# 98 of 8832 row tiles of a recommender kernel fetched row by row from ScalarE's queue

## The chip, the core and the metric

The kernel runs on one core of a Trainium2 chip. A core has five engines with instruction streams of their own: TensorE (PE), VectorE (DVE), ScalarE (ACT), GpSimd (POOL) and SyncE (SP). TensorE multiplies matrices and writes into PSUM. VectorE and ScalarE do elementwise work. DMAs between HBM and the on-chip memory are issued by GpSimd, SyncE or ScalarE and are carried by the core's 16 DMA engines. Engines wait for each other through semaphores. The metric is the time of one execution on the device in microseconds; lower is better.

## The reference

16384 samples have 69 item numbers each, and one label. Each item number picks a row of 96 float32 from a table of 100001 rows. Each row is weighted by a small network that looks at the row, the label's row and their difference and product; the weighted rows are summed in ten groups of fields (20, 20, 10, 10, 2, 2, 2, 1, 1, 1), and a network of three layers turns the sums into one number for each sample.

```python
u = emb[batch_user]
ql = emb[batch_label[:, 0]]
q = jnp.broadcast_to(ql[:, None, :], u.shape)
z = jnp.concatenate([q, u, q - u, q * u], axis=-1)
h = _dice(z @ W1 + b1, a1, EPS_DICE)
h = h @ W2 + b2
att = h @ W3 + b3
eff = (batch_user < ITEM_NUM)[..., None]
pre = jnp.where(eff, u * att, 0.0)
pooled = jnp.einsum('gf,bfe->bge', window, pre).reshape(u.shape[0], G * E)
x = jnp.concatenate([pooled, ql], axis=-1)
h = _dice(_bn_eval(x @ Wf1 + bf1, EPS_BN), af1, EPS_DICE)
h = _dice(_bn_eval(h @ Wf2 + bf2, EPS_BN), af2, EPS_DICE)
return h @ Wf3 + bf3
```

`_dice(x, a)` is (a (1 - p) + p) x with p the sigmoid of x. The 16384 x 69 = 1130496 picked rows are fetched as 8832 tiles of 128 rows.

## The kernel before

The samples are worked off in 32 blocks of 512. A block has 69 chunks of 512 rows (64 for the first 64 fields, five for the last five), a chunk has four tiles of 128 rows, and two chunks make a pair. There are 1104 pairs, and a step of the program's plan fetches one pair. The order of all instructions is written out by hand: `plan` (L528 to L587) holds for each step the pieces of work in the order in which each engine gets them, and the loop at L594 runs it. A step i of the long middle holds, in this order: every fourth step `attend_rows` and `spread` (attention weights of four earlier pairs), `hidden(i - 2)`, `pool(i - 7)`, `fetch(i)`. Pieces of the last network (`top1` to `top3`) and of the labels' rows (`head_gather`, `head_turn`, `head_rows`) are strewn in, block by block.

- `fetch` (L301) takes a buffer `u` of eight tiles (pool `upool`, 14 buffers). For each tile GpSimd issues one indirect DMA (`gather`, L257) that picks 128 rows of the table by the item numbers in `ids`, one row to a partition. TensorE transposes the tile into `ptr` (L313, PSUM, two buffers). When the four tiles of a chunk are transposed, VectorE multiplies `ptr` by the label's row into `quT` (L316 or L323), and ScalarE copies it to `uT` (L325); both must be done before the buffer of `ptr` is used again.
- `hidden` (L328) multiplies `uT` and `quT` by the first layer's weights into `ph` (L338, L342); ScalarE makes the sigmoid and an affine step (L344, L345), and VectorE the product `y` (L346).
- `pool` (L387) multiplies the rows in `u`, as they were fetched, by the attention weights (L397). After it the buffer of `u` is free for the pair 14 further on.
- `load_ids` (L144) loads the item numbers of four blocks at once, from SyncE, into one of two buffers, 20 steps before the first pair that needs them. `head_gather` (L271) adds four gathers a block for the labels' rows: 128 in all, 8960 gathers with the 8832.

Before the loop, constants are loaded from SyncE (`wn` at L153, `wf` at L155), and twelve copies of VectorE (L178) fill constant rows of the `uT` buffers.

Of the kernel before, what the change touches and what calls it, by code (L numbers as in the profile page):

```python
# [1 line left out]

# [7 lines left out]

F32 = mybir.dt.float32
I32 = mybir.dt.int32
AF = mybir.ActivationFunctionType
ALU = mybir.AluOpType
PSUM = bass.MemoryType.PSUM

P = 128
# [25 lines left out]
EARLY = 20  # L65

CLOSE = 8


class Pack:  # L70


    def __init__(self, **shapes):
        self.places, self.width = {}, 0
        for name, (row, n, m) in shapes.items():
            self.places[name] = slice(row, row + n), slice(self.width, self.width + m)
            self.width += m
# [37 lines left out]
def rec_kernel(  # L115
# [3 lines left out]
    idx: bass.AP,  # L119
    emb: bass.AP,  # L120
    rows: bass.AP,
    near: bass.AP,
    far: bass.AP,
    out: bass.AP,
):
    nc = tc.nc

    const = ctx.enter_context(tc.tile_pool(name="const", bufs=1))
    ipool = ctx.enter_context(tc.tile_pool(name="ipool", bufs=2))
# [14 lines left out]
    def load_ids(n):  # L144

        t = ipool.tile([P, NIDS, NCOL], I32, tag="ids", name=f"ids{n}")
        nc.sync.dma_start(out=t.rearrange("p b n -> p (b n)"), in_=idx[(n - 1) // NIDS])
        for k in range(NIDS):
            ids[n + k] = t[:, k, :]


    wn = const.tile([P, NEAR.width], F32, name="wn")
    nc.sync.dma_start(out=wn, in_=near)  # L153
# [102 lines left out]
    def gather(table, dst, index):  # L256
        nc.gpsimd.indirect_dma_start(  # L257
            out=dst,
            out_offset=None,
            in_=table,  # L260
            in_offset=bass.IndirectOffsetOnAxis(ap=index, axis=0),
        )

    def chunk(c):

        n, k = divmod(c, NCH)
        if n == NBLK - 1 and k >= EARLY:
            k = NMAIN + k - EARLY if k < EARLY + NTAIL else k - NTAIL
        return n, k

    def head_gather(n):  # L271

# [28 lines left out]
    def fetch(i, between=None):  # L301

        u = upool.tile([P, 8, E], F32, tag="u", name=f"u{i}")
        uT = []
        quT = tpool.tile([E, 2, 512], F32, tag="quT", name=f"quT{i}")
        for j in range(2):
            if j == 1 and between:
                between()
            n, k = chunk(2 * i + j)
            ptr = ps_tr.tile([E, 512], F32, tag="tr", name=f"ptr{i}_{j}")  # L310
            for t in range(4):
                gather(rows, u[:, 4 * j + t, :], ids[n][:, 4 * k + t : 4 * k + t + 1])
                nc.tensor.transpose(ptr[:, t * P : (t + 1) * P], u[:, 4 * j + t, :], ident)  # L313
            q = qTs[n % 2][0:E]
            if k < NMAIN:
                nc.vector.tensor_tensor(  # L316
                    quT[:, j, :].rearrange("e (s f) -> e s f", f=FM),
                    ptr.rearrange("e (s f) -> e s f", f=FM),
                    by_field(q[:, k * NS : (k + 1) * NS]),
                    ALU.mult,  # L320
                )
            else:
                nc.vector.tensor_tensor(quT[:, j, :], ptr, q[:, 0:BLK], ALU.mult)  # L323
            uT.append(room(k))
            nc.scalar.copy(uT[j][0:E], ptr)  # L325
        return u, uT, quT

    def hidden(i, uT, quT):  # L328

        ph = ps_h.tile([P, 512], F32, tag="h", name=f"ph{i}")  # L330
        places = [chunk(2 * i + j) for j in range(2)]
        sums = [ph[j * H1 : (j + 1) * H1, :] for j in range(2)]
        for (n, k), p in zip(places, sums):
            if k >= NMAIN:
                nc.tensor.matmul(p, Cq, qTs[n % 2], start=True, stop=False)  # L335
        for j, ((n, k), p) in enumerate(zip(places, sums)):
            if k < NMAIN:
                nc.tensor.matmul(p, As[n % 2][:, k // 4, :], uT[j], start=True, stop=False)  # L338
            else:
                nc.tensor.matmul(p, A, uT[j][0:E], start=False, stop=False)  # L340
        for j, p in enumerate(sums):
            nc.tensor.matmul(p, Wp, quT[:, j, :], start=False, stop=True)  # L342
        y = ypool.tile([P, 512], F32, tag="y", name=f"y{i}")
        nc.scalar.activation(y, ph, AF.Sigmoid, scale=S_DICE)  # L344
        nc.scalar.activation(y, y, AF.Identity, bias=a1c, scale=na1c)  # L345
        nc.vector.tensor_mul(y, ph, y)  # L346
        return y
# [9 lines left out]

    def attend_tail(i, j, y, uT):

        n, k = chunk(2 * i + j)  # L360
        pa = ps_x.tile([E, 512], F32, tag="x", name=f"pa{i}_{j}")
        nc.tensor.matmul(pa, vrep[j * H1 : (j + 1) * H1, :], y[j * H1 : (j + 1) * H1, :], start=True, stop=True)  # L362
        nc.vector.scalar_tensor_tensor(pres[n][:, k - NMAIN, :], pa, bb[0:E], uT[j][0:E], ALU.add, ALU.mult)  # L363
# [23 lines left out]
    def pool(i):  # L387

        u, rw = us.pop(i), rws.pop(i)
        todo = [(j, *chunk(2 * i + j)) for j in range(2)]  # L390
        todo = [(j, n, k) for j, n, k in todo if k < NMAIN]
        if not todo:
            return
        pa = ps_acc.tile([E, 2, NS, G], F32, tag="acc", name=f"acc{i}")
        for j, n, k in todo:
            for t in range(4):
                nc.tensor.matmul(  # L397
                    pa[:, j, 2 * t : 2 * t + 2, :].rearrange("e n g -> e (n g)"),
                    u[:, 4 * j + t, :],
                    rw[:, t, j, :],  # L400
                    start=True,
                    stop=True,
                )
        if len(todo) == 2:
            _, n, k = todo[0]
            nc.vector.tensor_copy(  # L406
                pooled[n][:, :, k * NS : (k + 2) * NS].rearrange("e g s -> e s g"),
                pa.rearrange("e j s g -> e (j s) g"),
            )
        else:  # L410
            j, n, k = todo[0]
            nc.vector.tensor_copy(
                pooled[n][:, :, k * NS : (k + 1) * NS].rearrange("e g s -> e s g"), pa[:, j]
            )
# [88 lines left out]
    def hidden_of(k):  # L503
        return lambda: ys.__setitem__(k, hidden(k, *hs[k]))

    def tails_of(k):
        def work():
            uT = hs.pop(k)[0]
            for j in range(2):
                if chunk(2 * k + j)[1] >= NMAIN:  # L510
                    attend_tail(k, j, ys[k], uT)

        return work

    def fetch_of(k, between=()):
        def work():
            for j in range(2):
                n = chunk(2 * k + j)[0]
                if n not in pooled:
                    pooled[n] = bpool.tile([E, G, BLK], F32, tag="pooled", name=f"pooled{n}")  # L520
                    pres[n] = xpool.tile([E, NTAIL, BLK], F32, tag="pre", name=f"pre{n}")
            u, uT, quT = fetch(k, lambda: [w() for w in between])
            us[k], hs[k] = u, (uT, quT)

        return work
# [4 lines left out]
    def at(step, *work):  # L530
        plan.setdefault(step, []).extend(work)

    c = NPAIR - CLOSE
    for i in range(c):
        if i >= 3 and (i - 3) % 4 == 3:
            at(i, rows_of(i - 6, 4))
        if i >= 3:
            at(i, tails_of(i - 3))
        if i >= 4 and (i - 4) % 4 == 3:
            at(i, spread_of(i - 7, 4))  # L540
        if i >= 2:
            at(i, hidden_of(i - 2))
        if i < c - CLOSE:
            if i >= POOL_LAG:
                at(i, pool_of(i - POOL_LAG))
        else:

            for k in {0: (-15, -14), 1: (-13,), 3: (-12, -11), 4: (-10, -9), 7: (-8, -7)}.get(i - c + 8, ()):
                at(i, pool_of(c + k))
        at(i, fetch_of(i))  # L550

    at(c, pool_of(c - 6), pool_of(c - 5), tails_of(c - 3), hidden_of(c - 2), fetch_of(c))
    at(c + 1, tails_of(c - 2), hidden_of(c - 1), fetch_of(c + 1))
# [7 lines left out]
    for n in range(NBLK):  # L561
        first, end = n * NCH // 2, ((n + 1) * NCH - 1) // 2
        if n > 0:
            if n % NIDS == 1:
                at(first - 20, lambda n=n: load_ids(n))
            at(first - 14, lambda n=n: qs.__setitem__(n, head_gather(n)))
            at(first - 11, lambda n=n: head_turn(n, qs.pop(n)))
            at(first - 9, lambda n=n: head_rows(n))
        if n < NBLK - 2:
            for s, work in enumerate(top_steps(n, slice(0, BLK))):  # L570
                at(end + POOL_LAG + 4 + s, work)
        elif n == NBLK - 2:
            for s, work in enumerate(top_steps(n, slice(0, BLK))):
                at(end + POOL_LAG + s // 2, work)
# [85 lines left out]
```

## Time and profile before

The three timed runs took 11247.6, 11251.05 and 11253.1 us; their median is 11251.05 us.

| What | Value |
|---|---|
| span of the profiled execution, first to last instruction | 11239.3 us |
| TensorE matmuls, busy | 9082.8 us, 81% |
| TensorE weight loads, busy | 4395.1 us, 39% |
| VectorE, busy | 3014.3 us, 27% |
| ScalarE, busy | 3188.3 us, 28% |
| GpSimd, busy | 8465.4 us, 75% |
| granted clock of TensorE, mean | 0.727 |
| gathers' queue, packets and share of the 16 DMA engines | 286720, 18.7% |
| a gather from issue to landing, median | 2.5 us |

Busy time leaves out what an engine spends on waiting, on register and semaphore work and, for SyncE and ScalarE, on issuing DMAs. The ends of matmuls are modelled, so that TensorE's 81% is an upper view of its load. A row of a group names the line, the engine, the operation, output and input, and the count; then the busy time and the mean of one in ns; then the idle time of the engine just ahead of these instructions, and what ended most of it. "issue" is idle time that no semaphore or transfer in the profile accounts for.

### The profile page before, as it was taken

The numbers are of one execution on the slowest core, as the hardware profiler recorded it, in microseconds if no ns is written. First come the engines' busy times: TensorE is split into PE (matmuls) and PEld (weight loads), VectorE is DVE, ScalarE is ACT, GpSimd is POOL, SyncE is SP. The second block draws the span as 40 slices with busy tenths as digits, with TensorE's granted clock in tenths as the row PEclk, the third lists the DMA queues.
The fourth block names the chain that finished last, engine by engine and source line by source line (L and its number), as shares of the span: only waits on it lengthen the run. The fifth ranks groups of instructions, "written<-read, shape, count | busy, mean of one in ns | idle before, by whom it ended". The sixth has DMA issues, their size and how long they took to land.

```text
span 11239.3 us, 108444 instructions
## 1 busy us (share of the span) xinstructions
PE 9082.8 (81%) x41797; PEld 4395.1 (39%) x41797; DVE 3014.3 (27%) x5325; ACT 3188.3 (28%) x4969; POOL 8465.4 (75%) x8966
## 2 busy tenths in 40 slices
PE   7888888888878787877888778777787887888888
PEld 3333433333433333333333333333343333433335
DVE  3222222222222222222222222222222222222222
ACT  2222222222222222222222222222222222222223
POOL 7777777777777777777777777777777777777776
PEclk6767777677776777777777777777777767777767
DMA  2111111111111111111111111111111111111111
GB/s 49 40 40 40 40 40 42 40 40 40 40 42 40 40 40 40 42 40 40 40 40 42 40 40 40 40 42 40 40 40 40 42 40 40 40 40 40 40 40 35
DMA packets 288946, 454.19 MB, mean 40 GB/s; under 512 B 143538, under 2 KB 143922, under 8 KB 288306
## 3 DMA queue, kind: packets, MB, share of 16 engines
q0 software_dynamic: 286720, 440.98, 18.7%
q8 instruction: 335, 5.49, 0.2%
q1 hardware_dynamic: 1714, 6.28, 0.2%
q14 instruction: 177, 1.45, 0.0%
HBM read 446.61 MB, written 0.07 MB: 40 GB/s over the span
## 4 chain that ended last, share of the span: by engine, by line
POOL 51%; issue 23%; PE 15%; DMA 11%; ACT 0%; DVE 0%; POOLq 0%
POOL u L257 50%; DMA u<-in_rows,ids 11%; PE p L438 4%; PE acc L397 3%; PE ph L342 2%; PE ph L338 2%; PE ptr L313 2%; POOL q L257 1%; PE prow L353 1%; PE ph L335 1%; PE ph L340 0%; PE pc L290 0%; PE pa L362 0%; PE patt L370 0%; PE p L449 0%
## 5 line engine op out<-in xcount | busy, mean ns | idle before, releaser
L257 POOL DMA_INDIRECT u<-in_rows,ids x8832 | 8343.6, 945 | 2690.9 <-issue 2510.2
L313 PE MATMUL ptr<-ident,u 128*96 128x128 f32 x8832 | 2092.4, 336 | 2080.2 <-DMA u<-in_rows,ids 2066.4
L325 ACT COPY uT<-ptr 96x512 f32<-96x512 f32 x2208 | 1285.2, 582 | 4422.4 <-DVE quT L316 4069.1
L313 PEld LDWEIGHTS ptr<-ident,u 128*96 128x96 f32 x8832 | 1184.6, 150 | 2904.1 <-DMA u<-in_rows,ids 2460.6
L397 PEld LDWEIGHTS acc<-rw,u 128*96 128x96 f32 x16384 | 1746.1, 190 | 1206.4 <-issue 1059.7
L346 DVE TENSOR_TENSOR y<-ph,y 128x512 f32<-128x512 f32 x1104 | 763.5, 692 | 4885.1 <-ACT y L345 4703.4
L316 DVE TENSOR_TENSOR quT<-ptr,qT 96x512 f32<-96x512 f32 x2048 | 1375.9, 677 | 2183.2 <-PE ptr L313 2180.0
L397 PE MATMUL acc<-rw,u 128*96 128x20 f32 x16384 | 1852.9, 260 | 23.1 <-DVE rw L375 18.0
L338 PE MATMUL ph<-uT,A 128*64 128x512 f32 x4096 | 1688.2, 902 | 1.0 <-ACT uT L325 1.0
L342 PE MATMUL ph<-quT,wn 96*64 96x512 f32 x4416 | 1628.4, 809 | 0.0
L344 ACT ACTIVATE y<-ph 128x512 f32<-128x512 f32 x1104 | 659.4, 597 | 2971.7 <-PE ph L342 2962.3
L345 ACT ACTIVATE y<-y,wn,na1c 128x512 f32<-128x512 f32 x1104 | 898.1, 814 | 37.3
L342 PEld LDWEIGHTS ph<-quT,wn 96*64 96x64 f32 x4416 | 447.5, 191 | 1070.4 <-issue 1069.8
L438 PE MATMUL p<-pooled,wf 96*100 96x512 f32 (+1 forms) x1400 | 706.2, 654 | 0.0
L338 PEld LDWEIGHTS ph<-uT,A 128*64 128x64 f32 x4096 | 269.0, 179 | 616.0 <-issue 609.8
L406 DVE COPY pooled<-acc 96x160 f32<-96x160 f32 x1008 | 419.9, 417 | 129.4 <-PE acc L397 129.4
L353 PE MATMUL prow<-y,v 128*32 128x512 f32 x2208 | 452.4, 894 | 0.3 <-DVE y L346 0.3
L438 PE MATMUL p<-pre,V 96*100 96x512 f32 (+1 forms) x700 | 398.9, 717 | 2.7 <-DVE x L421 2.3
L438 PEld LDWEIGHTS p<-pooled,wf 96*100 96x100 f32 x1400 | 265.6, 202 | 341.2 <-issue 341.2
L375 DVE SCALAR_TENSOR_TENSOR rw<-patt,bb,wn 128x320 f32<-128x320 f32 x554 | 277.8, 543 | 221.2 <-PE patt L370 220.3
L355 ACT COPY row<-prow 128x512 f32<-128x512 f32 (+1 forms) x277 | 161.8, 584 | 314.5 <-PE prow L353 314.2
L370 PE MATMUL patt<-ident,row 128*128 128x128 f32 x1108 | 231.2, 347 | 15.9 <-DVE pre L363 15.2
(66 smaller groups left out, 2227.6 us busy)
## 6 DMA issues: line engine op xcount, KB each, us to landing
u<-in_rows,ids POOLq DMA_INDIRECT x8832, 2.5
ids<-in_idx SPq DMA_DIRECT2D x8, 560.0 KB, 3.7
q<-in_emb,ids POOLq DMA_INDIRECT x128, 2.5
wf<-in_far SPq DMA_DIRECT2D x1, 1209.0 KB, 7.8
wn<-in_near SPq DMA_DIRECT2D x1, 236.0 KB, 2.7
ids<-in_idx SPq DMA_DIRECT2D x1, 140.0 KB, 2.2
out<-r SPq DMA_DIRECT2D x1, 63.5 KB
out<-r SPq DMA_DIRECT2D x1, 0.5 KB
```

Of the source, the lines that this page charges most:

```text
L257: nc.gpsimd.indirect_dma_start(out=dst, out_offset=None, in_=table, in_offset=bass.IndirectOffsetOnAxis(ap=index, axis=0),)
L313: nc.tensor.transpose(ptr[:, t * P : (t + 1) * P], u[:, 4 * j + t, :], ident)
L316: nc.vector.tensor_tensor(quT[:, j, :].rearrange("e (s f) -> e s f", f=FM), ptr.rearrange("e (s f) -> e s f", f=FM), by_field(q[:, k * NS ...
L325: nc.scalar.copy(uT[j][0:E], ptr)
L338: nc.tensor.matmul(p, As[n % 2][:, k // 4, :], uT[j], start=True, stop=False)
L342: nc.tensor.matmul(p, Wp, quT[:, j, :], start=False, stop=True)
L344: nc.scalar.activation(y, ph, AF.Sigmoid, scale=S_DICE)
L345: nc.scalar.activation(y, y, AF.Identity, bias=a1c, scale=na1c)
L346: nc.vector.tensor_mul(y, ph, y)
L353: nc.tensor.matmul(pr[32 * k : 32 * (k + 1), :], v2, ys[b + k], start=True, stop=True)
L397: nc.tensor.matmul(pa[:, j, 2 * t : 2 * t + 2, :].rearrange("e n g -> e (n g)"), u[:, 4 * j + t, :], rw[:, t, j, :], start=True, stop=True,)
L438: nc.tensor.matmul(p1, w[:, h * DH : (h + 1) * DH], x, start=(k == 0), stop=(k == KTOP - 1))
```

## The change

98 of the 8832 tiles are no longer fetched by an indirect DMA of GpSimd. They are the last tile (slot 3) of the second chunk of the pairs 15, 26, 37 and so on, one in eleven pairs, up to pair 1082. ScalarE issues 128 DMAs for each, one for each row of 384 bytes, into a buffer of its own (`ring`, three buffers of 128 x 384 bytes).

The byte offsets of the rows come from a new input, `single_rows`, a 64 KB array of item numbers that SyncE loads ahead of `wn`; VectorE multiplies it by 384 in two operations. ScalarE loads offsets into registers, 24 at a time (8 at a tile's end), and uses each as the address of one DMA. A tile's rows are issued over eleven steps, twelve a step (eight in the last), and end three steps before the step that transposes the tile. Within a step six rows are issued ahead of `pool` and `fetch`, which on ScalarE is after the sigmoid and affine step of `hidden(i - 2)`, and six after `fetch`, which is after its two copies to `uT`. Row DMAs count up one of eight semaphores. In place of the gather's landing TensorE waits for that semaphore ahead of the transpose; the transpose and `pool` read the ring's buffer instead of `u`. The buffer of `u` keeps its eight places.

The item numbers of four blocks are loaded 50 steps ahead in place of 20. `chunk` becomes `chunk_of`, outside the kernel's function, with the same content.

```diff
+ROW_BYTES = 4 * E
+SLOT = 3
+SP_CHUNKS = []
+SP_RING = 0
+ACT_CHUNKS = [2 * (11 * s + 15) + 1 for s in range(98)]
+ACT_RING = 3
+ACT_ROWS = 12
+ACT_STEPS = -(-P // ACT_ROWS)
+SINGLES = SP_CHUNKS + ACT_CHUNKS
+NSB = (len(SINGLES) + P - 1) // P
+NSEM = 8
...
+    row_bytes = rows.bitcast(U8).rearrange("(o n) k -> o (n k)", o=1)
...
+    offsets = const.tile([P, NSB, P], I32, name="offsets")
+    nc.sync.dma_start(out=offsets.rearrange("p b r -> p (b r)"), in_=single_rows)
+    nc.vector.tensor_scalar(offsets, offsets, 3, None, ALU.mult)
+    nc.vector.tensor_scalar(offsets, offsets, 7, None, ALU.logical_shift_left)
...
+        def load(self, s, start):
+
+            i, stop = self.first + s, min(P, start + self.group)
+            _, values = nc.values_load_multi_w_load_instructions(
+                offsets[i % P : i % P + 1, i // P, start:stop],
+                engines=[self.kind],
...
+            self.values = dict(enumerate(values, start))
+
+        def fetch(self, s, start, stop):
+
+            b, k = self.buffers[s % len(self.buffers)], s % NSEM
+            for r in range(start, stop):
+                if r % self.group == 0:
+                    self.load(s, r)
+                d = self.engine.dma_start(
+                    out=ring[r : r + 1, b], in_=row_bytes[:, bass.ds(self.values[r], ROW_BYTES)]
+                ).then_inc(self.sems[k], 16)
...
+            if stop == P:
+                for ins in fresh.pop(b):
+                    tc.add_to_no_dep_group(f"ring{b}", ins)
+                self.given[k] += 16 * P
+                places[self.chunks[s]] = b, self.sems[k], self.given[k]
...
+    def single(c, t):
+        return places.get(c) if t == SLOT else None
+
+    def wait_for_single(c, t):
+        if single(c, t):
+            nc.tensor.wait_ge(*single(c, t)[1:])
+
+    def read_rows(op, out, u, c, t, other, **how):
+
+        at = single(c, t)
+        ins = op(out, ring[:, at[0]].bitcast(F32) if at else u[:, 4 * (c % 2) + t, :], other, **how)
...
             for t in range(4):
-                gather(rows, u[:, 4 * j + t, :], ids[n][:, 4 * k + t : 4 * k + t + 1])
-                nc.tensor.transpose(ptr[:, t * P : (t + 1) * P], u[:, 4 * j + t, :], ident)
+                if single(2 * i + j, t):
+                    wait_for_single(2 * i + j, t)
+                else:
+                    gather(rows, u[:, 4 * j + t, :], ids[n][:, 4 * k + t : 4 * k + t + 1])
+                read_rows(nc.tensor.transpose, ptr[:, t * P : (t + 1) * P], u, 2 * i + j, t, ident)
...
+    by_scalar = Singles(
+        "act",
+        nc.scalar,
+        mybir.EngineType.Activation,
+        ACT_CHUNKS,
+        len(SP_CHUNKS),
+        range(SP_RING, SP_RING + ACT_RING),
+        2 * ACT_ROWS,
+    )
+    turn = {}
+    for s, m in enumerate(ACT_CHUNKS):
+        for k in range(ACT_STEPS):
+            turn.setdefault(m // 2 - 2 - ACT_STEPS + k, []).append((s, k * ACT_ROWS, min(P, (k + 1) * ACT_ROWS)))
+
+    def scalar_rows(i, half):
+
+        for s, start, stop in turn.get(i, []):
+            middle = min(stop, start + ACT_ROWS // 2)
+            if half == 0:
+                by_scalar.fetch(s, start, middle)
+            elif middle < stop:
+                by_scalar.fetch(s, middle, stop)
...
             at(i, hidden_of(i - 2))
+        at(i, lambda i=i: scalar_rows(i, 0))
...
         at(i, fetch_of(i))
+        at(i, lambda i=i: scalar_rows(i, 1))
...
-                at(first - 20, lambda n=n: load_ids(n))
+                at(max(0, first - 50), lambda n=n: load_ids(n))
```

More of the change, by code (lines that the diff above doesn't have):

```diff
@@ L34 @@
 I32 = mybir.dt.int32
+U8 = mybir.dt.uint8
 AF = mybir.ActivationFunctionType
@@ L67, with chunk_of @@
 CLOSE = 8
+ROW_BYTES = 4 * E
[9 more added lines that the diff above has]
+NSEM = 8
+def chunk_of(c):
+    n, k = divmod(c, NCH)
+    if n == NBLK - 1 and k >= EARLY:
+        k = NMAIN + k - EARLY if k < EARLY + NTAIL else k - NTAIL
+    return n, k
 class Pack:
@@ L121, in rec_kernel @@
     rows: bass.AP,
+    single_rows: bass.AP,
     near: bass.AP,
@@ L124, in rec_kernel @@
     out: bass.AP,
+    ring: bass.AP,
 ):
     nc = tc.nc
+    row_bytes = rows.bitcast(U8).rearrange("(o n) k -> o (n k)", o=1)
     const = ctx.enter_context(tc.tile_pool(name="const", bufs=1))
@@ L262, in gather, with __init__ @@
         )
[L264 to L269, printed above, removed]
+    places = {}
+    class Singles:
+        def __init__(self, name, engine, kind, chunks, first, buffers, group):
+            self.name, self.engine, self.kind, self.group = name, engine, kind, group
+            self.chunks, self.first, self.buffers = chunks, first, buffers
+            self.sems = [tc.alloc_semaphore(f"{name}{k}") for k in range(NSEM)]
+            self.given = [0] * NSEM
+        def load(self, s, start):
[3 more added lines that the diff above has]
+                engines=[self.kind],
+                min_val=0,
+                max_val=ITEM_NUM * ROW_BYTES,
+                skip_runtime_bounds_check_because="offsets of rows of the table",
+            )
[8 more added lines that the diff above has]
+                ).then_inc(self.sems[k], 16)
+                tc.no_tile_sem_insts.add(d.ins.name)
+                tc.declare_no_dep(d.ins, group=f"ring{b}", reason="a buffer's readers have waited for its rows")
+                fresh.setdefault(b, []).append(d.ins)
+            if stop == P:
[3 more added lines that the diff above has]
+                places[self.chunks[s]] = b, self.sems[k], self.given[k]
@@ L271, in head_gather @@
+    fresh = {}
+    def single(c, t):
[6 more added lines that the diff above has]
+        ins = op(out, ring[:, at[0]].bitcast(F32) if at else u[:, 4 * (c % 2) + t, :], other, **how)
+        if at:
+            tc.declare_no_dep(ins.ins, group=f"ring{at[0]}", reason="waited for by semaphore")
     def head_gather(n):
@@ L308, in fetch @@
                 between()
-            n, k = chunk(2 * i + j)
+            n, k = chunk_of(2 * i + j)
             ptr = ps_tr.tile([E, 512], F32, tag="tr", name=f"ptr{i}_{j}")
             for t in range(4):
-                gather(rows, u[:, 4 * j + t, :], ids[n][:, 4 * k + t : 4 * k + t + 1])
-                nc.tensor.transpose(ptr[:, t * P : (t + 1) * P], u[:, 4 * j + t, :], ident)
+                if single(2 * i + j, t):
[3 more added lines that the diff above has]
+                read_rows(nc.tensor.transpose, ptr[:, t * P : (t + 1) * P], u, 2 * i + j, t, ident)
             q = qTs[n % 2][0:E]
@@ L330, in hidden @@
         ph = ps_h.tile([P, 512], F32, tag="h", name=f"ph{i}")
-        places = [chunk(2 * i + j) for j in range(2)]
+        places = [chunk_of(2 * i + j) for j in range(2)]
         sums = [ph[j * H1 : (j + 1) * H1, :] for j in range(2)]
@@ L358, in attend_tail @@
     def attend_tail(i, j, y, uT):
-        n, k = chunk(2 * i + j)
+        n, k = chunk_of(2 * i + j)
         pa = ps_x.tile([E, 512], F32, tag="x", name=f"pa{i}_{j}")
@@ L389, in pool @@
         u, rw = us.pop(i), rws.pop(i)
-        todo = [(j, *chunk(2 * i + j)) for j in range(2)]
+        todo = [(j, *chunk_of(2 * i + j)) for j in range(2)]
         todo = [(j, n, k) for j, n, k in todo if k < NMAIN]
@@ L396, in pool @@
             for t in range(4):
-                nc.tensor.matmul(
+                read_rows(
+                    nc.tensor.matmul,
                     pa[:, j, 2 * t : 2 * t + 2, :].rearrange("e n g -> e (n g)"),
-                    u[:, 4 * j + t, :],
+                    u,
+                    2 * i + j,
+                    t,
                     rw[:, t, j, :],
@@ L509, in work @@
             for j in range(2):
-                if chunk(2 * k + j)[1] >= NMAIN:
+                if chunk_of(2 * k + j)[1] >= NMAIN:
                     attend_tail(k, j, ys[k], uT)
@@ L517, in work @@
             for j in range(2):
-                n = chunk(2 * k + j)[0]
+                n = chunk_of(2 * k + j)[0]
                 if n not in pooled:
@@ L531, in at @@
         plan.setdefault(step, []).extend(work)
+    by_scalar = Singles(
[6 more added lines that the diff above has]
+        2 * ACT_ROWS,
+    )
+    turn = {}
[9 more added lines that the diff above has]
+                by_scalar.fetch(s, middle, stop)
     c = NPAIR - CLOSE
@@ L620, in side_by_side @@
         return a.reshape(n, -1, a.shape[1]).transpose(1, 0, 2).reshape(-1, n * a.shape[1])
+    singles = np.zeros((P, NSB, P), np.int32)
+    for s, m in enumerate(SINGLES):
+        n, k = chunk_of(m)
+        singles[s % P, s // P] = ids[n][:, 4 * k + SLOT]
     arrays = {
@@ L626 @@
         "rows": np.concatenate([x["emb"][:ITEM_NUM], np.zeros((1, E), np.float32)], axis=0),
+        "single_rows": singles.reshape(P, -1),
         "near": NEAR.fill(
@@ L655 @@
     out = nc.dram_tensor("out_0", (B, 1), F32, kind="ExternalOutput").ap()
+    ring = nc.alloc_sbuf_tensor("ring", [P, SP_RING + ACT_RING, ROW_BYTES], U8).ap()
     with tile.TileContext(nc) as tc:
-        rec_kernel(tc, *args, out)
+        rec_kernel(tc, *args, out, ring)
     r = run_bass_kernel_spmd(nc, [arrays], core_ids=[0])
```

## The prediction

> **What bounds the kernel now.** I read the page first: its chain of waits, its groups, its DMA queues. Then the timeline of GpSimd for the pace of the gathers, and the timeline of SyncE for the price of a DMA that a hardware queue issues. The chain, and the two groups behind it:
>
> ```profile
> POOL 51%; issue 23%; PE 15%; DMA 11%; ACT 0%; DVE 0%; POOLq 0%
> L257 POOL DMA_INDIRECT u<-in_rows,ids x8832 | 8343.6, 945 | 2690.9 <-issue 2510.2
> L313 PE MATMUL ptr<-ident,u 128*96 128x128 f32 x8832 | 2092.4, 336 | 2080.2 <-DMA u<-in_rows,ids 2066.4
> ```
>
> 74% of the chain is GpSimd making gathers and the pause between two of them. The second row gives 945 ns of work and 2690.9/8832 = 0.305 us of idle ahead of each gather. The third shows that TensorE waits for the landing of gathers (2066.4 us), not the other way round. The same is seen in the timeline of GpSimd in the middle of the run:
>
> ```profile
> 5601.77 0.94 POOL L257 DMA_INDIRECT u<-in_rows,ids  x1 [0.30 <-issue]
> 5603.02 0.94 POOL L257 DMA_INDIRECT u<-in_rows,ids  x1 [0.30 <-issue]
> 5604.27 0.94 POOL L257 DMA_INDIRECT u<-in_rows,ids  x1 [0.30 <-issue]
> ```
>
> and among all its waits in the list of waits, of which the last column is the longest:
>
> ```profile
> POOL u L257 <- issue: 2510.2, 8239, 0.3
> POOL u L257 <- DMA u<-in_rows,ids: 120.7, 396, 0.3
> POOL u L257 <- PE ptr L313: 43.6, 143, 0.3
> POOL u L257 <- PE acc L397: 7.3, 24, 0.3
> ```
>
> No gather ever waited more than 0.3 us: the name in each row only says whose signal fell into a pause that was there anyway. GpSimd never blocks. From the first u gather (start 8.37 us) to the last (start 11196.52) lie 11188.15 us and 8831 + 124 gathers (the 124 are those of L275 after block 0): **1.2494 us each**. After the last gather come some 42 us of TensorE and the store. So the kernel is 8960 gathers in single file with a short tail, and the other engines have room.
>
> **What the Trainium skill says.** "DMA: Bandwidth & Descriptors", under SWDGE vs HWDGE vs iDMA (its part on issuing engines), holds that DMAs of ScalarE, SyncE and GpSimd run on the same 16 DMA engines, and that issuing from several saves the sequencer's issue time alone. Here that time is what bounds: the gathers' queue takes 18.7% of the 16 engines, by the page. "Perfetto Trace Analysis", DMA Instruction — HWDGE, says that the recorded time of such a DMA is the sequencer's, descriptors included, after which it takes its next instruction; the rows of SyncE below agree (0.41 us each, the next 0.05 us later). The same page, DVE / Act Engine Instruction, says that an ACTIVATE is pushed into a queue in front of the engine, where its semaphore wait is served, and the sequencer goes on. If so, rows can be issued while an operation waits or runs; no trace here shows it for ScalarE, and I don't need it below.
>
> **The change, part by part.**
>
> *Removed.* The order of the built program has 8862 gathers on GpSimd in place of 8960. 98 x 1.2494 = 122.4 us off the file. Nothing is put on GpSimd, and a lone missing gather leaves no hole, as the next one waits for nothing but its pause.
>
> *Rows on ScalarE.* 98 x 128 = 12544 DMAs of 384 bytes, in the steps from 2 to 1079, 12 a step (8 in the eleventh), on average 128/11 = 11.64. They stand in two bunches of six: after the sigmoid pair of a step (L344, L345), and after its two copies (L325). ScalarE issues no DMA before, so I price one from SyncE:
>
> ```profile
> 0.75 0.41 SPq L142 DMA_DIRECT2D ids<-in_idx  x1
> 1.21 0.42 SPq L153 DMA_DIRECT2D wn<-in_near  x1
> 1.68 0.42 SPq L155 DMA_DIRECT2D wf<-in_far  x1
> 1761.06 0.33 SPq L147 DMA_DIRECT2D ids<-in_idx  x1
> 11237.14 0.25 SPq L474 DMA_DIRECT2D out<-r  x1
> ```
>
> The last moves one row of 0.5 KB in 0.25 us, a later load of 128 partitions takes 0.33, the first ones 0.42, with 0.05 between. Bounds for a row: 0.30 and 0.47 us. I take 0.35, between the one-row store and the later load with the gap, as the address comes from a register: 11.64 x 0.35 = 4.1 us a step (3.5 to 5.5).
>
> *Register loads.* Six a tile, five of 24 offsets and one of 8, hence 6/11 = 0.55 a step. No trace shows one. Prices: "DMA: Bandwidth & Descriptors", Latency and other measured facts, has 0.6 us as a floor for one (0.33 us a step); "Runtime: NRT & Kernel Launch", Instruction fetch mechanics, has about 0.2 us a register, which for 128 registers in eleven steps is 2.33 us a step as an estimate; that is for registers filled from HBM, here they come from SBUF. I take 1.3, the middle.
>
> *Does it fit?* ScalarE is busy 3188.3 us in 1104 steps, 2.9 us each. With nothing overlapped: 2.9 + 4.1 + 1.3 = 8.3 us, against a step of (8960/1104 - 98/1078) x 1.2494 = 10.03 us. So it is hidden with 1.7 us to spare. If that cover were gone, every us over costs 1078 us.
>
> *Lateness within a step.* Queued behind a bunch (2.1 us, plus a load in every second step) are the copies that free ptr, and behind the other bunch the next sigmoid. ptr has two buffers, and a chunk's transposes need the copy of the same half one step earlier, nearly 10 us before; hidden runs two steps behind fetch. And if TensorE does slip: u has 14 buffers and is pooled 7 steps later, so GpSimd may lead TensorE by nearly 7 steps, some 70 us, before it blocks. Only a lasting shortage on ScalarE or TensorE can reach it. TensorE has 96 new waits, for rows whose last bunch stands three steps ahead of the transpose that uses them (a gather lands in 2.5 us). Behind such a wait stand the transpose and all of TensorE's following work; I cost it at nothing, and the same 70 us cover it.
>
> *DMA engines.* 12544 small transfers. A gather leaves 286720/8960 = 32 packets; if a row left as many, each as long as the mean one of the gathers' queue (0.187 x 16 x 11239/286720 = 0.117 us), they would take 26% of the 16 engines. 19 + 26 = 45% at most: time to landing may grow, not the pace of GpSimd, which waits for no landing.
>
> *Start, ids, end.* One more 64 KB load stands ahead of wn and wf on SyncE (0.46 us), and two operations on VectorE wait for it; GpSimd needs only ids and starts as before, and TensorE may be 14 pairs behind at the start. The ids loads go 30 steps earlier into a double buffer. The last rows are issued 25 steps before the end; the tail of 42 us stays. Nothing for all three.
>
> *Sum.* Against the profiled execution: 11239.3 - 122.4 = 11116.9 us. The median of the runs is 11251.05, 11.75 above that span, for what lies around it. **Forecast: 11128.6, so 11129 us.**
>
> **The rivals.**
>
> *A. Forecast: ScalarE keeps up, gathers keep their pace.* For it: every row above. Its own range is 11118 to 11142, the repeat runs' spread of a few us and a ns or so a gather. Chance 0.68.
>
> *B. ScalarE becomes the bound (slower).* Place: its instruction stream in the steps 2 to 1079. At the upper prices, nothing overlapped, a step costs 2.9 + 11.64 x 0.47 + 2.33 = 10.7 us, 0.67 above 10.03: 1078 x 0.67 = 722, so 11851 us. It decides once the three terms pass 10.03: rows at 0.41 us with the dearest loads, or at 0.58 with the cheapest. For it: the first three SyncE rows, and that one load holds up to 24 registers. Against it: SyncE's 0.25 and 0.33 later in the run, and that both dear prices must hold with no overlap. Chance 0.11.
>
> *C. The gathers get slower.* 8862 gathers give the whole gain back at 122.4/8862 = 13.8 ns each. For it: the four gathers started from 13.36 to 17.48 us, beside the twelve VectorE copies at L178, take 1.04 to 1.09 us in the timeline, so their making can be disturbed. Against it: while the ids load of 1761 us lands, DMA share 0.36 in place of 0.19 from 1760 to 1770 us, they stay at 0.94. At 5 ns each: 44 us, 11173. If the rows disturbed as those copies do, for the 40% of the time in which they are issued: 0.125 x 0.4 x 8862 = 443 us, 11572. Chance 0.21, of which 0.12 stays below 11228, 0.04 near no change, 0.05 slower.
>
> *D. It does not do what it says* (the gathers stay on GpSimd): ruled out by the count of 8862.
>
> **How the numbers follow.** A change of 0.2%, 22.5 us, is about what a measurement of this kernel tells from none: 11228.5 to 11273.6. Faster: A 0.68 + C 0.12 = 0.80. Same: 0.04. Slower: B 0.11 + C 0.05 = 0.16. The range goes from A's lower end to 11230, the end of C's faster part: 0.80 in it.
>
> **What would show it right or wrong.** Right: GpSimd at 945 ns a gather with pauses of 0.30 us and 98 fewer; ScalarE's row DMAs near 0.3 us; TensorE still waiting for gathers; the chain still mostly GpSimd. B would show as waits of GpSimd for TensorE well over 0.3 us, and TensorE waiting for ScalarE's copies at L313. C would show as a mean above 950 ns or a longer pause. The forecast falls if a row's issue or a register load costs far more than SyncE's rows suggest, or if gathers stretch by over 10 ns.

## The result and the profile after

Four runs each, beside each other: 11252.08 us before (11247.6 to 11253.46), 11126.92 us after (11126.51 to 11132.1). The ratio is 0.9892, with a 95% interval of 0.9878 to 0.9906: 125.2 us less, where 122.4 had been forecast, and 11127 us for 11129. The profiled execution has a span of 11124.7 us, 114.6 us less than the one before; why that is less than the medians' difference is told with the prediction's sum, below.

The page of the changed kernel: first its chain of waits, then the group of the gathers (the row for L257 before), the group of transposes (L313 before) and the one of ScalarE's copies (L325 before). The columns are as before: count, busy time and mean in ns, idle time ahead and what ended it.

```profile
POOL 48%; issue 20%; PE 17%; DMA 14%; ACT 0%; DVE 0%; ACTq 0%; POOLq 0%
...
L266 POOL DMA_INDIRECT u<-in_rows,ids x8734 | 8262.1, 946 | 2663.9 <-issue 2429.1
L325 PE MATMUL ptr<-ident,u 128*96 128x128 f32 x8734 | 2047.4, 335 | 2012.5 <-DMA u<-in_rows,ids 1993.2
L386 ACT COPY uT<-ptr 96x512 f32<-96x512 f32 x2208 | 1268.0, 582 | 4448.8 <-DVE quT L377 3312.6
```

There are 98 gathers fewer, their length and the pause ahead of them (2663.9/8734 = 0.305 us) are what they were, and TensorE still waits for gathers for 1993.2 us. ACTq, the sequencer of ScalarE that issues the rows, has 0% of the chain. The list of waits has no wait of GpSimd for TensorE above 0.3 us (last column), so GpSimd still never blocks (but for 1.9 us at the start, before as after, until the first item numbers have landed):

```profile
POOL u L266 <- issue: 2429.1, 7964, 0.3
POOL u L266 <- DMA u<-in_rows,ids: 173.8, 570, 0.3
POOL u L266 <- PE ptr L325: 43.0, 141, 0.3
```

What the rows cost is in two lists by tile, of `ring` and of `offsets` (shortest, median and longest duration in ns, then first and last start):

```profile
L301 ACTq MOVE ring<-in_rows x12544: 29/29/29, 36.7 to 10861.2; - x200
L301 ACTq DMA_DIRECT2D ring<-in_rows x12544: 213/213/503, 36.8 to 10861.2; - x200
L286 ACTq TENSOR_LOAD <-offsets x588: 717/1677/1739, 34.9 to 10857.9; - x196
```

A row is a register move of 29 ns, which the source does not name, and a DMA issue of 213 ns. A stretch of ScalarE's timeline has both kinds of bunches (start, length, engine, line, operation; in brackets the idle time ahead):

```profile
5603.68 0.58 ACT L386 COPY uT<-ptr 96x512 f32<-96x512 f32 x1 [1.93 <-DVE quT L377]
5603.75 1.74 ACTq L301 DMA_DIRECT2D ring<-in_rows  x6
5606.58 0.60 ACT L405 ACTIVATE y<-ph 128x512 f32<-128x512 f32 x1 [2.31 <-PE ph L403]
5607.21 0.81 ACT L406 ACTIVATE y<-y,wn,na1c 128x512 f32<-128x512 f32 x1
5607.28 1.74 ACTq L301 DMA_DIRECT2D ring<-in_rows  x6
```

Six rows take 1.74 us, 0.29 each with the gaps. A bunch begins 0.07 us after the *start* of the operation ahead of it and runs beside it. From 1000 to 9080 us this timeline holds some 1735 stretches of rows that follow an operation of ScalarE. Of these, 1060 begin within 0.12 us of its start, and some 355 begin 1.8 to 1.9 us after it, which leaves room for a register load of 1.7 us ahead of the first row (such a load starts at 5619.0 us). But the copy of the first line had waited 1.93 us for VectorE, and the rows had waited with it. The row list of the DMA queues has, for the rows:

```profile
q10 hardware_dynamic: 25088, 4.87, 0.3%
```

Two packets a row, and 0.3% of the 16 engines.

### The profile page after: what moved, and what is told of

The parts are those of the page before. It is cut to its first block, busy times and chain, and to the rows that moved or that the text cites. A ratio compares the mean times of both kernels' runs of the same rounds, so it can differ in the third digit from the quotient of the medians.

```text
span 11124.7 us, 134126 instructions
## 1 busy us (share of the span) xinstructions
PE 9017.1 (81%) x41797; PEld 4375.5 (39%) x41797; DVE 3007.2 (27%) x5327; ACT 3171.0 (29%) x4969; POOL 8384.0 (75%) x8868
## 4 chain that ended last, share of the span: by engine, by line
POOL 48%; issue 20%; PE 17%; DMA 14%; ACT 0%; DVE 0%; ACTq 0%; POOLq 0%
POOL u L266 47%; DMA u<-in_rows,ids 14%; PE p L502 4%; PE acc L325 3%; PE ph L403 2%; PE ph L399 2%; PE ptr L325 2%; POOL q L266 1%; PE prow L414 1%; PE pa L423 1%; PE ph L396 0%; PE ph L401 0%; PE pc L348 0%; PE patt L431 0%; PE p L513 0%
## 5 line engine op out<-in xcount | busy, mean ns | idle before, releaser
L266 POOL DMA_INDIRECT u<-in_rows,ids x8734 | 8262.1, 946 | 2663.9 <-issue 2429.1
L325 PE MATMUL ptr<-ident,u 128*96 128x128 f32 x8734 | 2047.4, 335 | 2012.5 <-DMA u<-in_rows,ids 1993.2
L325 PEld LDWEIGHTS ptr<-ident,u 128*96 128x96 f32 x8734 | 1170.4, 150 | 2798.6 <-DMA u<-in_rows,ids 2364.7
L325 PEld LDWEIGHTS acc<-rw,u 128*96 128x96 f32 x16200 | 1719.7, 189 | 1210.7 <-issue 1038.1
L325 PE MATMUL acc<-rw,u 128*96 128x20 f32 x16200 | 1826.3, 260 | 39.7 <-DVE rw L436 34.0
```

The source lines that it names most:

```text
L266: nc.gpsimd.indirect_dma_start(out=dst, out_offset=None, in_=table, in_offset=bass.IndirectOffsetOnAxis(ap=index, axis=0),)
L325: ins = op(out, ring[:, at[0]].bitcast(F32) if at else u[:, 4 * (c % 2) + t, :], other, **how)
```

## The experiments

Runs of one group were made on one chip beside the kernel before, which took 11252 us in the group of the result, 13463 us in one group that is told of below, and 11230 to 11231 us in the others; so ratios are compared.

**Rows without the gain, and the gain without rows.** In the first kernel all 8960 gathers are made as well, and nothing reads the ring.

```diff
-                if single(2 * i + j, t):
-                    wait_for_single(2 * i + j, t)
-                else:
-                    gather(rows, u[:, 4 * j + t, :], ids[n][:, 4 * k + t : 4 * k + t + 1])
+                wait_for_single(2 * i + j, t)
+                gather(rows, u[:, 4 * j + t, :], ids[n][:, 4 * k + t : 4 * k + t + 1])
...
-        at = single(c, t)
+        at = None
```

> All 8960 gathers stay on GpSimd, and ScalarE issues the same 12544 row DMAs into the ring, which nothing reads; TensorE still waits for their semaphore. Theory 1 (the file of gathers on GpSimd is all that counts, rows are free): as before, 11252 us, within 5 us. Theory 2 (rows stretch the gathers a little: the profile after has a pace of 1.2510 us in place of 1.2494, 1.6 ns more): 8960 x 1.6 ns = 14 us more, 11266. Theory 3 (much of the gain does not come from the gathers taken away, but from what else the change moved: the earlier loads of ids, other waits): clearly below 11252, towards 11127.

Measured: 11230.34 us against 11229.93, ratio 1.0000, interval 0.9992 to 1.0008. The 12544 rows, their loads and their waits, together with what else the change moved, cost or bring nothing beyond this interval, some 9 us each way.

In the second kernel the rows are left out instead:

```diff
-        if single(c, t):
-            nc.tensor.wait_ge(*single(c, t)[1:])
+        pass
...
-        ins = op(out, ring[:, at[0]].bitcast(F32) if at else u[:, 4 * (c % 2) + t, :], other, **how)
...
+        ins = op(out, blank if at else u[:, 4 * (c % 2) + t, :], other, **how)
...
-        at(i, lambda i=i: scalar_rows(i, 0))
...
-        at(i, lambda i=i: scalar_rows(i, 1))
```

> The 98 tiles are neither gathered nor fetched by rows: their transposes and products read one constant tile, so the fetch of 98 tiles is left out of the computation. Theory 1: the same as the changed kernel, 11127 us within 5, as the rows cost nothing. Theory 2 (rows stretch the gathers by 1.6 ns): 8862 x 1.6 ns = 14 us less, 11113, and a pace of 1.2494 us a gather in the profile. If rows made TensorE or ScalarE late in a way that counts, lower still.

Measured: 11105.67 us, ratio 0.9889 (0.9874 to 0.9904), against 0.9892 with the rows. So the gain is that of the 98 gathers: 124.3 us here, 1.27 each. The two runs together also leave little room for a cost of the rows that something else in the change makes good, as the rest of the change is in this run and the rows are not. The theory that rows stretch gathers by 1.6 ns falls with the first run, where its 14 us lie outside the interval. The second run points the same way (139 us less by that theory, 124.3 measured), but its interval alone doesn't exclude it. The pace that had suggested it came from single profiled executions, and these differ: in the first run the profiled one took 11255.44 us, the other twelve 11226 to 11234 us.

**Where does ScalarE's stream end?** More tiles by rows, with the same bunches grown.

```diff
-ACT_CHUNKS = [2 * (11 * s + 15) + 1 for s in range(98)]
+ACT_CHUNKS = [2 * (6 * s + 15) + 1 for s in range(178)]
-ACT_ROWS = 12
+ACT_ROWS = 22
-NSEM = 8
+NSEM = 16
...
-        2 * ACT_ROWS,
+        24,
```

The other two have 134 tiles, one in eight steps, 16 rows, and 214 tiles, one in five, 26 rows.

> One tile in eight steps in place of eleven: 134 tiles, 16 rows a step. Sum for ScalarE with nothing overlapped, from the prices in the profile after: 2.9 + 16 x 0.29 + 9.1/8 = 8.7 us a step, under the step of GpSimd, (8960/1104 - 1/8) x 1.25 = 9.99. Theory 1: 11252 - 134 x 1.2494 = 11085 us. A rival, by which a late ScalarE already costs time below its limit: the gain per tile falls below 1.25 us, so above 11090.

Measured: 11065.41 us, ratio 0.9853 (0.9837 to 0.9868), 164.5 us less, 1.23 a tile.

> One tile in six steps: 178 tiles, 22 rows a step. GpSimd alone: 11252 - 178 x 1.2494 = 11030 us, steps of 9.94 us. ScalarE with nothing overlapped: 2.9 + 21.3 x 0.29 + 9.1/6 = 10.6 us a step, 0.65 over, so 11030 + 1068 x 0.65 = 11720 us, slower than before. If rows are issued beside the running operation ahead of them (the bunches in the profile after begin 0.07 us after the start of a copy or of the affine step, which hides 0.5 and 0.75 us a step): 9.3 us a step, it fits, 11030 us.

Measured: 11009.88 us, ratio 0.9803 (0.9788 to 0.9818), 220 us less, 1.24 a tile. The sum without overlap had 10.6 us a step and forecast 11720: it is wrong. ScalarE's timeline in this run shows why it just fits:

```profile
6010.66 0.58 ACT L386 COPY uT<-ptr 96x512 f32<-96x512 f32 x1 [4.90 <-issue]
6010.76 0.52 ACTq L301 DMA_DIRECT2D ring<-in_rows  x2
6011.14 0.58 ACT L386 COPY uT<-ptr 96x512 f32<-96x512 f32 x1
6011.37 2.64 ACTq L301 DMA_DIRECT2D ring<-in_rows  x9
6014.06 0.60 ACT L405 ACTIVATE y<-ph 128x512 f32<-128x512 f32 x1 [2.33 <-PE ptr L325]
6014.69 0.81 ACT L406 ACTIVATE y<-y,wn,na1c 128x512 f32<-128x512 f32 x1
6014.75 5.32 ACTq L301 DMA_DIRECT2D ring<-in_rows  x11
6020.12 0.58 ACT L386 COPY uT<-ptr 96x512 f32<-96x512 f32 x1 [4.62 <-issue]
```

From copy to copy this common step takes 9.46 us, and the stream is without a hole: an operation starts 0.05 us after the row ahead of it, and rows run beside the copies and the affine step; two of them even begin ahead of the second copy, which at 6010.76 stands in line behind the first one. (The 5.32 us of eleven rows hold a register load, which has no row here.) GpSimd's step is 9.94 us. A step with rarer operations is longer: the next one, with two of the last network, takes 10.87 us. ACTq has 10% of this run's chain, and TensorE waits 173.5 us for copies at its transposes, 3.0 us in the changed kernel; but no wait of GpSimd is above 0.3 us. One step further it can't fit:

> One tile in five steps: 214 tiles, 26 rows a step. In the run with one tile in six steps ScalarE's stream was seen full, 9.5 to 9.7 us a step with nothing between, of which 6.4 + 1.5 us were rows and loads and some 1.7 the operations that rows don't overlap. Here rows and loads take 25.6 x 0.29 + 9.1/5 = 9.2 us, with 1.7 and 0.4 for the rarer operations 11.3 a step against 9.89 of GpSimd. Theory ScalarE's stream as the limit (rival B of the prediction): GpSimd's 10963 (11230 - 214 x 1.245) plus 1070 x 1.4 = 12460 us, slower than before by 11%, and GpSimd waits for TensorE. Theory the gathers alone count: 10963 us.

Measured: 12453.91 us, ratio 1.1092 (1.1074 to 1.1111). The chain of waits, and the waits of GpSimd, have changed hands:

```profile
ACTq 65%; issue 15%; ACT 10%; PE 8%; DVE 1%; POOL 1%; DMA 0%; DVEq 0%
```

```profile
POOL u L266 <- PE ptr L325: 1132.7, 435, 15.9
POOL u L266 <- PE acc L325: 509.2, 152, 15.2
```

GpSimd now waits for TensorE to free buffers of `u`, up to 15.9 us at a time. ScalarE's register loads start from 94.8 to 12187.9 us, over 1070 steps of 11.3 us, the step that had been summed. This is the slower rival of the prediction, reached by more rows and not by dearer ones.

**Is lateness within a step free?** All twelve rows of a step in one bunch, ahead of the copies:

```diff
-            middle = min(stop, start + ACT_ROWS // 2)
+            middle = stop
```

> The changed kernel with all twelve rows of a step in one bunch ahead of the copies to uT, in place of six and six. The copies then come 3.5 us late, 5.2 with a load. Theory: lateness within a step is absorbed by the two steps between fetch and hidden and by the 14 buffers of u, so as the changed kernel: 0.989 of before. Rival: bunching matters, as TensorE waits for a free ptr; then TensorE's transposes wait for copies, and the gain falls below half, ratio above 0.994.

Measured: 11107.96 us, ratio 0.9890 (0.9873 to 0.9906). The first line below is of the changed kernel, the others are of this run. ScalarE's idle time ahead of copies that no semaphore explains grows from 806.6 to 2490.7 us, TensorE's waits for copies at its transposes only from 3.0 to 23.9 us, and none of it arrives at GpSimd:

```profile
ACT uT L386 <- issue: 806.6, 264, 3.4
...
ACT uT L386 <- issue: 2490.7, 640, 5.3
...
POOL u L266 <- issue: 2305.9, 7564, 0.3
```

Two bunches of six were not needed at this rate.

**Does it matter who issues?** The 178 tiles by SyncE, in chunks that are first in their pair, with a ring of four:

```diff
+    by_sync = Singles("sp", nc.sync, mybir.EngineType.SP, SP_CHUNKS, 0, range(SP_RING), 24)
...
+    def sync_rows(i):
+        for s, start, stop in sp_turn.get(i, []):
+            by_sync.fetch(s, start, stop)
...
+        at(i, lambda i=i: sync_rows(i))
```

> The 178 tiles (one in six steps) by rows of SyncE instead of ScalarE, 24 rows behind each load, in a ring of four; ScalarE issues none. Theory: it is only the number of gathers left, whoever issues the rows: as the run with 178 tiles by ScalarE, 0.980 of before, 11010 us. SyncE needs 128 x 0.29 + 9.1 = 46 us a tile and has 6 x 9.94 = 60. Rival: SyncE's rows in long runs of 24 crowd the DMA engines or the gathers' landing, then above 0.985.

Measured: 11008.03 us, ratio 0.9801 (0.9784 to 0.9817), the same as by ScalarE.

**Both queues.** As there, and ScalarE issues too; `u` has 13 buffers.

> 178 tiles by SyncE and 134 by ScalarE (one in eight steps), 312 in all; u has 13 buffers in place of 14 to make room for the rings (five and three). Theory: GpSimd still bounds, 11230 - 312 x 1.245 = 10842 us, 0.965 of before. Rival: TensorE is the next bound, as its idle ahead of the transposes shrinks from 2066 us before by some 390 us, and with 13 buffers GpSimd begins to wait: above 10880.

Measured: 10842.84 us, ratio 0.9655 (0.9639 to 0.9671), 388 us less than before; by the ratio of the changed kernel, 0.9892, that is 267 us below it. TensorE still waits for gathers:

```profile
POOL 48%; issue 20%; PE 17%; DMA 13%; ACTq 1%; ACT 1%; DVE 0%; POOLq 0%; DVEq 0%
...
L325 PE MATMUL ptr<-ident,u 128*96 128x128 f32 x8520 | 2000.6, 336 | 1786.1 <-DMA u<-in_rows,ids 1752.6
```

One more notch on both, 214 tiles by SyncE and 178 by ScalarE:

> 214 tiles by SyncE (one in five steps) and 178 by ScalarE (one in six), 392 in all; u has 13 buffers, rings of six and three. Theory: GpSimd still bounds, 11231 - 392 x 1.245 = 10743 us, 0.9565 of before. ScalarE's stream takes 9.5 to 9.7 us a step, as in the run with 178 tiles by ScalarE alone, while the step of GpSimd shrinks to (8960/1104 - 1/5 - 1/6) x 1.245 = 9.65. Rival: ScalarE's stream now decides, at 9.7 us a step and more where rare operations fall in, above 10760 us, and GpSimd waits for TensorE.

Measured: 11430.38 us, ratio 1.0180 (1.0163 to 1.0197): a miss, and for neither of the two reasons. The chain, and the list by tile of `ring`:

```profile
SPq 67%; issue 17%; ACTq 8%; PE 4%; ACT 2%; POOL 1%; DMA 1%; DVE 0%; POOLq 0%
```

```profile
L301 SPq MOVE ring<-in_rows x27392: 29/29/29, 7.1 to 11202.8; - x200
L301 SPq DMA_DIRECT2D ring<-in_rows x27392: 227/228/493, 7.1 to 11202.9; - x200
```

SyncE takes 0.228 us for an issue, and in the chain its rows stand 0.32 us apart in place of the 0.29 that I had carried over from ScalarE. From its first to its last row, 11195.8/214 = 52.3 us a tile, and five steps of GpSimd have 48. SyncE is the bound, and the rows come late: TensorE waits 1301.7 us for `ring`. To tell that from rows of two queues hindering each other, SyncE's share was taken back to one in six. The first two runs of this, one of them with a smaller share for ScalarE too, were on a chip where even the kernel before took 13463 us and a register move took up to 1.48 us:

> 178 tiles by SyncE (one in six steps) and 153 by ScalarE (one in seven), 331 in all; u has 13 buffers. In the run with 392 tiles a row of SyncE took 0.32 us and a tile 52.3 us, more than five steps of 9.65; six steps have 58. ScalarE: 18.3 x 0.29 + 9.1/7 + 2.1 = 8.7 us a step against (8960/1104 - 1/6 - 1/7) x 1.245 = 9.72 of GpSimd. Theory (the slowest of three issuing streams decides, and here that is GpSimd): 11231 - 331 x 1.245 = 10819 us, 0.963 of before. Rival: two streams of rows hinder each other or the gathers from some rate on, and the run with 392 tiles was slow for that: above 10843, the time with 312 tiles.

> 178 tiles by SyncE and 178 by ScalarE, each one in six steps, 356 in all. SyncE has 58 us for 52.3. GpSimd's step is (8960/1104 - 2/6) x 1.245 = 9.69 us, and ScalarE's stream took 9.5 to 9.7 in common steps, and more where rare operations fall in. Theory of the slowest stream: if ScalarE's mean stays under 9.69, 11231 - 356 x 1.245 = 10788 us; if it is 9.8 to 10.0, 10900 to 11100. Above 11230 only if the two streams of rows hinder each other, as SyncE is not the limit here.

Measured there: 15989.47 us (331 tiles) and 16057.99 us (356 tiles), ratios 1.1883 and 1.1932. Gathers had their 944 ns, but register moves and DMA issues of SyncE and ScalarE often took 0.7 us and more. What disturbed that chip is not known; these two runs say nothing on the question. Once more, on a chip like those of the other groups:

> The kernel with 178 tiles by SyncE and 178 by ScalarE once more, as the chip of the last call took 13463 us for the kernel before and single register moves there took up to 1.5 us. Against the run with 392 tiles only SyncE's share is changed, from one in five steps to one in six. If SyncE's stream (52.3 us a tile) was the limit there, fewer tiles by rows make the kernel faster: GpSimd alone 11231 - 356 x 1.245 = 10788 us; with ScalarE's mean step at up to 10.0 us in place of 9.69, up to 11120. If the number of rows from two queues was what hurt, it stays near 11400.

Measured: 10858.43 us, ratio 0.9664 (0.9648 to 0.9680). 36 tiles fewer by rows make the kernel 572 us faster. SyncE's longest waits ahead of its rows say why; the first line is of the run with 392 tiles, the second of this one:

```profile
SPq L301 <- PE ptr L325: 3.8, 16, 0.3
...
SPq L301 <- PE acc L325: 1086.6, 147, 18.5
```

With 392 tiles SyncE hardly ever waited; now it waits 1086.6 us for buffers of the ring to come free, and TensorE no longer waits for `ring`. So SyncE's stream was the limit. The time stays 70 us above what GpSimd alone would give. The chain says which stream does that, and GpSimd waits for TensorE again, up to 8.2 us at a time:

```profile
ACTq 61%; issue 14%; PE 12%; ACT 11%; POOL 1%; DVE 1%; DMA 0%; POOLq 0%; DVEq 0%
...
POOL u L266 <- PE ptr L325: 84.0, 111, 8.2
```

The run with 312 tiles has the lowest time of all, though its interval overlaps that of this run, and there GpSimd still bounds.

## Why the prediction was right

- *The file of gathers.* 98 times 1.2494 us was shown from both ends: gathers put back, all of the gain gone; rows left out, all of it kept. From 98 to 312 tiles, as long as GpSimd bounds, the gain is 1.23 to 1.28 us for each.
- *The sum's last step.* The prediction put 11.75 us between the span and the runs down to "what lies around it". In the runs that list both, the time lies only 1.8 us above the span. The profiled execution before was thus, by estimate, some 10 us quicker than the median of the timed ones, which is also why the two profiled spans differ by only 114.6 us. The forecast doesn't suffer, as the same amount stands on both sides. That it came within 2 us is luck in part: the interval of the ratio is some 16 us each way.
- *A row at 0.35 us* (0.30 to 0.47): it took 0.29, just under the lower bound. The one-row store of SyncE was the right neighbour to look at; the loads of 128 partitions were not.
- *Register loads at 1.3 us a step*: five of 1.68 and one of 0.72 us are 9.1 us a tile, 0.83 a step. For 24 registers, the 0.2 us each of the Trainium skill ("Runtime: NRT & Kernel Launch", Instruction fetch mechanics), which are for registers filled from HBM, would give 4.8 us as an estimate, and the floor of "DMA: Bandwidth & Descriptors", Latency and other measured facts, is 0.6. The trace lies between, and it decides.
- *The sum of 8.3 us without overlap* is 2.9 + 3.4 + 0.8 = 7.1 with these prices, and was not the limit. It is too high as a model too: at 22 rows a step it forbids what ran. With no need of the overlap at twelve rows, leaving it out was safe. The Trainium skill ("Perfetto Trace Analysis", DVE / Act Engine Instruction) states that the sequencer goes on once an operation is queued. The traces agree in part. Behind a copy that runs, or that only stands behind another copy, rows go ahead: in the run with 22 rows a step, from 1000 to 9000 us, they begin before the second copy in 706 of some 805 steps. Behind the copy at 5603.68, which had waited 1.93 us for VectorE, the rows had waited too. And between a sigmoid and its affine step, which reads what the sigmoid writes, no row begins in that stretch; the nearest begin with the affine step. Why the sequencer stands still there, no run shows.
- *Lateness within a step* at nothing: shown with the single bunch, ahead of whose copies ScalarE's unexplained idle time is three times as long. The cover of the `u` buffers is seen with 22 rows a step, where TensorE waits 173.5 us for copies and GpSimd for none of it.
- *The new waits of TensorE* at nothing: right as well. The prediction counts 96, but the source makes one for each of the 98 tiles. Ahead of these 98 transposes TensorE was idle for 0.0 us (the last figure):

```profile
L325 PE MATMUL ptr<-ident,ring 128*96 128x128 f32 x98 | 34.2, 349 | 0.0
```

- *DMA engines*: the bound of 26% was far too wide. A row is two packets, not 32, and takes 0.3% of the engines.
- *Rival B* was real and its place right: 26 rows a step bring it, at 1.109. *Rival C* did not happen: in the run with 22 rows a step gathers have a mean of 944 ns. *Rival D* fell with the count.

## What to carry to other kernels

When one engine makes the same instruction in single file and waits for nothing, as GpSimd here, the gain of taking one away is its start-to-start spacing, and the question is only whether the stream that takes the work has room. Add up that stream, issue by issue, with prices of the same queue and not of a neighbour, against the step of the bound: here 9.46 us in a common step of 9.94 cost nothing, and 11.3 of 9.89 made the kernel 11% slower. A full stream of issues did not show as busy time (ScalarE is busy 25% of the span with 26 rows a step); look for it in the chain of waits under its sequencer (ACTq, SPq), and in a timeline without holes.

## What the runs showed of the hardware

- A one-row DMA of 384 bytes with its address in a register has a move of 29 ns and an issue of 213 ns on ScalarE, 228 ns on SyncE. The spacing is 0.29 us on ScalarE and 0.32 us on SyncE. I had expected SyncE, which does nothing else, to be no slower.
- A load of 24 registers from on-chip memory took 1.68 us and one of 8 took 0.72: the two give 60 ns a register and 0.24 us besides, as an estimate. With 22 rows a step and more, the load of 24 took 1.78 us on ScalarE.
- 312 tiles by rows from two queues, 39936 small DMAs, left the gathers at 944 ns.
